# A graph-attention kernel on one core: three blocks of whole-array work in a batch, weights begun inside the last of them, the last batch's small work spread

## The chip, the core and the metric

The kernel runs on one NeuronCore of a Trainium2 chip. A core has five engines that run side by side, each through its own list of instructions: TensorE (PE, matrix products and transposes), VectorE (DVE), ScalarE (ACT), GpSimd (POOL) and SyncE (SP), which issues most of the DMAs. The metric is the time of one execution on the device in microseconds. Everything is float32.

## What is computed

Two layers, each followed by a residual addition and a layernorm. Layer 0 is a graph attention over 16 batches of 1024 nodes with 256 channels; layer 1 is a graph convolution with two linear layers and two batchnorms. The change lies in layer 0:

```python
fea = jnp.transpose(x, (0, 2, 1))
c_adj = jnp.mean(fea, axis=1)
diff = c_adj[:, None, :] - c_adj[:, :, None]
A = jnp.abs(jnp.abs(jax.nn.sigmoid(diff) - 0.5) - 0.5) * 2.0
A_s = (A + jnp.transpose(A, (0, 2, 1))) * 0.5
Wg = adj[None, :, :] * A_s
g = jax.nn.relu(jnp.einsum('bcn,bnm->bcm', fea, Wg) * para.reshape(1, C, N))
# q is g seen as 4 heads of 64 channels; k and v are the halves of x @ kv_w
attn = jax.nn.softmax(jnp.einsum('bhnd,bhmd->bhnm', q, k) * scale, axis=-1)
out = jnp.einsum('bhnm,bhmd->bhnd', attn, v)
x = _layernorm(x + out)
```

The weights of the graph depend on the differences of the nodes' channel means alone. In the kernel they come out as (tanh(|mean_i - mean_j| / 2) - 1) times the adjacency, and the sign goes into the scale of the queries.

## The kernel before, in words

Layer 0 is the first two thirds of the execution. Its work is a list of 512 units, 32 in a batch: batch b, pair of heads pr, half of the queries qh, and block m of 128 keys. Two units make a burst; a batch has 16 bursts, numbered u = 0 to 15. The two heads of a pair and the two halves of a key block are placed on the four 64 by 64 quadrants of TensorE, which compute side by side. For every burst the order is: `scores` (L903) of both its units into two score tiles of the "s" pool (two tiles of two PSUM banks each), each followed by its Exp on ScalarE (L908); then `back`, that is `outputs` (L924), of the burst before, whose additions of the exponentials to `acc` run on VectorE (L931, L933). So an Exp has the time of one `outputs` until the next scores want its tile. After the last key block the two output banks are put together in `oT` (ACT L937, then DVE L938).

All else on TensorE uses the whole 128 by 128 array, and is put between the bursts by hand: the order of TensorE, VectorE and ScalarE is exactly that of the program (`manual_schedule`). `prologue(b)` makes three lists for a batch, which are worked off one and two batches ahead:

- `first`: four transposes of x into xT (L765, with the copy L768). Ahead of the first stands `begin`: the channel sums (L747), the means and the negative means, a DMA that writes the 1024 negative means to DRAM (`c`, L754), and a second one that reads them back spread over all partitions (`crow`, L756). The second waits on SyncE until the first has landed.
- `steps`: the values (L855, 4 steps) and keys (L842, 4 steps), and `graph_mm` (L805, 16 steps), which multiplies x by the weights, half of the width at a time, into one-bank tiles of the "t" pool. After the last step of a half follow the product with `para` (DVE L814) and a Relu (ACT L817).
- `side`: the weights; for each of eight row blocks an Abs (L784) and a Tanh (L789) on ScalarE and a product with the adjacency (DVE L793). Abs reads `crow`. The eight weight tiles are freed by the last `graph_mm` that reads them.

`FULL` names the bursts with whole-array work: u = 0 and 4 take four steps of values and keys each, with two side steps after each; u = 6, 8, 10 and 12 take four steps of `graph_mm`; the transposes of `first` stand around those of u = 10 and 12. The remaining side steps stand at u = 13, 14, 15, 1, 2 and 3. The block of u = 6 is the first half width of the first 128 channels, and so on to u = 12.

Three dictionaries keyed by the burst hold what follows a pair of heads: `normalise` (L946 and L952: the denominators, four 128 by 32 products, copied and sent through DRAM into columns, L954 and L959) one burst later, `residual` (L967 to L979: reciprocal, transposes of oT, product, addition to x on POOL) five bursts later, and `finish_x1` six bursts later: `layernorm` wholly on VectorE (L596 to L600), with its square root on POOL, and a store of x1 by POOL. At u = 5, `load_x` reads the batch after the next into the slot of x that this store has freed.

In the last batch there is nothing to prepare. `last` puts there the transposes of the adjacency for layer 1 and other preparations; `before_last` puts row sums and the diagonal of the adjacency on VectorE in the batch before.

Of the kernel before, what the change touches and what calls it, by code (L numbers as in the profile page):

```python
# [18 lines left out]
P = 128  # L19
# [496 lines left out]
def fast_path(  # L516
# [86 lines left out]

    def products(name, bank, out, mm, temps, bias):
# [95 lines left out]
    with (  # L700
# [5 lines left out]
        tc.tile_pool(name="op", bufs=3) as op,  # L706
# [26 lines left out]
        def prologue(b):  # L733
# [24 lines left out]
            def transpose_x(c, half):  # L758
                if c == 0 and half == 0 and b:
                    begin()  # L760
# [7 lines left out]
                nc.vector.tensor_copy(s["xT"][:, c, half * HALF : (half + 1) * HALF], pt)  # L768
# [28 lines left out]
            def graph_mm(c, half, part):  # L797
                if part == 0:
                    s["pg"] = tile_t(f"pg_{b}_{c}_{half}")
                    if c == 0 and half == 0:  # L800
                        s["qT"] = qkv.tile([P, CC, N], F32, tag="qT", name=f"qT_{b}")
                ps = s["pg"]
                hs = slice(half * HALF, (half + 1) * HALF)
                for n in (2 * part, 2 * part + 1):
                    nc.tensor.matmul(  # L805
                        ps, xt[:, n, c * P : (c + 1) * P], s["wg", n][:, hs],
                        start=(n == 0), stop=(n == NCH - 1),
                    )
                if part == 3:
                    queries(c, hs, ps)  # L810
# [37 lines left out]
            def values(pair):  # L848
# [3 lines left out]
                for j in range(2):  # L852
# [6 lines left out]
                nc.vector.tensor_copy(  # L859
                    s["v"][:, 2 * pair : 2 * pair + 2, :].rearrange("p n c -> p (n c)"), pt  # L860
                )
# [3 lines left out]
            if b == 0:  # L865
                first += [(begin, ()), (row_of_means, ())]
            for i in range(4):
                step(values, i)
                step(keys, i // 2, i % 2)
            for c in range(CC):  # L870
                for half in range(2):
                    for part in range(4):
                        if b:
                            step(graph_mm, c, half, part)
# [105 lines left out]

        def finish_x1(b):
            xt = st.pop(b)["x"]
            layernorm(xt, f"l0_{b}")
            nc.gpsimd.dma_start(x1_d[b], xt)
# [125 lines left out]

        BURST = 2
        bursts = [range(i, i + BURST) for i in range(0, len(units), BURST)]
        PERB = PER // BURST
        FULL = (0, 4, 6, 8, 10, 12)
        SIDE = {13: 2, 14: 2, 15: 2, 1: 2, 2: 2, 3: 2}
        with tc.manual_schedule(engines={mybir.EngineType.PE, mybir.EngineType.Activation, mybir.EngineType.DVE}):
# [8 lines left out]
            run(next_first, 4)  # L1125
# [7 lines left out]
            full, sums, late = {}, {}, {}  # L1133

            def back(j):
# [4 lines left out]
                if m == NCH - 1 and qh == 1:  # L1140
                    sums.setdefault(j + 1, []).append((normalise, (b, pr)))
                    for q in range(2):
                        full.setdefault(j + 5, []).append((residual, (b, pr, q)))
                    if pr == PAIRS - 1:
                        late.setdefault(j + 6, []).append((finish_x1, (b,)))
# [14 lines left out]
                6: [(adjacency_rows, (n,)) for n in (0, 1, 2)] + [(load_weights, ())],  # L1160
                8: [(adjacency_rows, (n,)) for n in (3, 4, 5)],
                10: [(adjacency_rows, (n,)) for n in (6, 7)],
                12: [(adjacency_diagonal, ())],
            }
            for j in range(len(bursts)):
# [8 lines left out]
                run(late.get(j, []), 9)  # L1174
# [3 lines left out]
                if u in FULL:  # L1178
                    if u >= 10:
                        run(next_first, 1)  # L1180
                    for _ in range(4 if b or u > 4 else 0):
                        run(steps, 1)
                        if u <= 4:
                            run(side, 2)
                    if u >= 10:
                        run(next_first, 1)
                    run(full.get(j, []), 9)
                elif u > 12:
                    run(next_side, SIDE[u])
                else:  # L1190
# [441 lines left out]
```

## Time and profile before

| | us |
|---|---|
| median of three runs | 2638.08 (2633.52 to 2638.3) |
| the profiled execution's own time | 2637.64 |
| span of its trace | 2635.9 |
| TensorE idle within the span | 63.2 |
| scores L903, TensorE busy | 490.5 |
| outputs L924, TensorE busy | 485.3 |
| graph_mm L805, TensorE busy | 425.2 |
| Exp L908, ScalarE busy, mean of one | 495.6, 1.020 |
| additions L933, VectorE busy, mean of one | 483.2, 1.258 |
| weights L784 and L789, ScalarE busy | 146.6 and 135.5 |
| product with adjacency L793, mean of one | 1.217 |
| layernorm on VectorE: L596, L597, L600, mean of one | 0.397, 0.181, 0.407 |

The span runs from the first to the last instruction of the trace; the execution's own time also has what lies around it. The busy time of a group is the time in which at least one of its instructions ran. A matmul shows as two records, and the ends of matmuls are modelled, so their starts are what to compare. From 200 to 1600 us every stretch of 100 us looks alike: TensorE 99.4 busy, VectorE 62 to 69, ScalarE 50 to 55. Layer 0 ends near 1740 us; a batch takes 104.9 us (the write of the means L754 starts at 652.51, 757.42, 862.32 and 967.23).

### The profile page before, as it was taken

The page shows a single profiled execution, that of the slowest core. Times are in us where ns is not written, and L with a number is a line of the kernel's source. Part 1 is how long each engine was busy: PE and PEld are TensorE (multiplying, and loading weights), DVE is VectorE, ACT ScalarE, POOL GpSimd, SP SyncE. Part 2 cuts the span into 40 slices and gives each one's busy share as a digit, 9 for nine tenths or more (in the row PEclk, how much of TensorE's full clock was granted, in tenths as well). Part 3 has the DMA queues.
Part 4 walks back from the last instruction along what each step waited for, and adds up shares of the span by engine and source line. Part 5 has one row for each costly group of instructions (what it writes and reads, how often), then busy time and mean ns, then how long its engine had stood idle before and what let it go on. Part 6 is the DMA issues. An engine that isn't in the chain of part 4 may idle for free. (4 is left out here: it accounts for less than half of the span.)

```text
span 2635.9 us, 32325 instructions
## 1 busy us (share of the span) xinstructions
PE 2572.7 (98%) x13158; PEld 1118.6 (42%) x13158; DVE 1587.8 (60%) x2159; ACT 1110.2 (42%) x1321; POOL 338.9 (13%) x407
## 2 busy tenths in 40 slices
PE   8999999999999999999999999999999999999986
PEld 4443444444434444444344443334444444444455
DVE  5465665756656657566566576766565565533367
ACT  5363563644635636546356364501100111133358
POOL 0001000100000001001000010232221122000036
PEclk9999999999999999999999999999999999999999
DMA  4001101011011010110110110112222222254458
GB/s 144 2 9 41 33 10 41 17 25 33 9 41 33 10 41 19 23 33 9 41 33 9 41 49 2 41 55 89 96 76 84 86 90 96 96 201 150 159 194 303
DMA packets 134557, 168.96 MB, mean 64 GB/s; under 512 B 86784, under 2 KB 120064, under 8 KB 124032
## 3 DMA queue, kind: packets, MB, share of 16 engines
q1 hardware_dynamic: 129568, 116.47, 14.1%
q0 software_dynamic: 4832, 50.34, 4.6%
q8 instruction: 105, 1.72, 0.3%
q14 instruction: 52, 0.43, 0.0%
HBM read 99.36 MB, written 67.44 MB: 63 GB/s over the span
## 5 line engine op out<-in xcount | busy, mean ns | idle before, releaser
L908 ACT ACTIVATE p<-ps 128x1024 f32<-128x1024 f32 x512 | 495.6, 1020 | 179.7 <-PE ps L903 132.6
L933 DVE TENSOR_TENSOR acc<-acc,p 128x1024 f32<-128x1024 f32 x384 | 483.2, 1258 | 60.9 <-ACT p L908 32.3
L903 PE MATMUL ps<-qT,kT 64*64 64x512 f32 x4096 | 490.5, 594 | 1.4 <-ACT p L908 1.4
L924 PE MATMUL po<-p,v 64*64 64x512 f32 x4096 | 485.3, 589 | 0.0
L805 PE MATMUL pg<-wg,x 128*128 128x512 f32 x960 | 425.2, 596 | 0.0
L979 POOL TENSOR_TENSOR x<-x,o 128x512 f32<-128x512 f32 x64 | 109.5, 1711 | 1434.8 <-DVE o L974 1434.8
L924 PEld LDWEIGHTS po<-p,v 64*64 64x64 f32 x4096 | 156.7, 133 | 282.8 <-issue 282.6
L805 PEld LDWEIGHTS pg<-wg,x 128*128 128x128 f32 x960 | 177.6, 190 | 226.9 <-issue 203.3
L903 PEld LDWEIGHTS ps<-qT,kT 64*64 64x64 f32 x4096 | 146.1, 132 | 280.2 <-issue 231.5
L817 ACT ACTIVATE qT<-qT 128x512 f32<-128x512 f32 x64 | 40.1, 630 | 481.9 <-DVE qT L814 481.9
L1457 PE MATMUL po<-hl,w12T 128*128 128x512 f32 x512 | 222.0, 596 | 3.6 <-ACT hl L1387 2.8
L814 DVE SCALAR_TENSOR_TENSOR qT<-pg,para_s 128x512 f32<-128x512 f32 x64 | 43.9, 689 | 270.7 <-PE pg L805 269.8
L793 DVE SCALAR_TENSOR_TENSOR wg<-wg,adj_s 128x1024 f32<-128x1024 f32 x128 | 153.1, 1217 | 16.0 <-ACT wg L789 16.0
L1457 PEld LDWEIGHTS po<-hl,w12T 128*128 128x128 f32 x512 | 97.7, 191 | 127.9 <-issue 120.4
L784 ACT ACTIVATE wg<-crow,ccol 128x1024 f32<-128x1024 f32 x128 | 146.6, 1146 | 12.2 <-DMA crow<-c 12.2
L789 ACT ACTIVATE wg<-wg 128x1024 f32<-128x1024 f32 x128 | 135.5, 1059 | 2.6
L1387 ACT ACTIVATE hl<-hl,bn_sh,bn_sg 128x1024 f32<-128x1024 f32 x64 | 74.4, 1229 | 137.4 <-DMA hl<-h 136.1
L855 PE MATMUL pv<-kvw_s,xT 128*128 128x256 f32 x512 | 124.0, 385 | 1.6 <-ACT kT L846 1.6
L1468 DVE TENSOR_SCALAR o<-po,col_b 128x1024 f32<-128x1024 f32 x31 | 39.8, 1283 | 138.1 <-PE po L1457 138.1
L842 PE MATMUL pk<-xT,kvw_s 128*128 128x512 f32 x256 | 120.3, 592 | 0.0
L855 PEld LDWEIGHTS pv<-kvw_s,xT 128*128 128x128 f32 x512 | 94.9, 190 | 51.9 <-issue 27.6
L1286 PE MATMUL b_agg<-aT,x1S 128*128 128x512 f32 x240 | 109.2, 598 | 0.0
(159 smaller groups left out, 2641.4 us busy)
## 6 DMA issues: line engine op xcount, KB each, us to landing
h<-hw POOLq DMA_DIRECT2D x16, 2048.0 KB, 6.6
hl<-h SPq DMA_DIRECT2D x15, 2048.0 KB
x<-x POOLq DMA_DIRECT2D x16, 1024.0 KB, 4.2
x1l<-x SPq DMA_DIRECT2D x16, 1024.0 KB
xf<-x SPq DMA_DIRECT2D x16, 1024.0 KB
out_dram<-o SPq DMA_DIRECT2D x16, 1024.0 KB
x<-in_x_dram SPq DMA_DIRECT2D x15, 1024.0 KB
crow<-c SPq DMA_DIRECT2D x15, 512.0 KB
```

Source lines behind the costliest of these rows:

```text
L784: nc.scalar.activation(w, s["crow"], AF.Abs, bias=s["ccol"][:, n : n + 1])
L789: nc.scalar.activation(w, w, AF.Tanh, scale=0.5)
L793: nc.vector.scalar_tensor_tensor(w, w, 1.0, adj_s[:, n, :], op0=ALU.subtract, op1=ALU.mult)
L805: nc.tensor.matmul(ps, xt[:, n, c * P : (c + 1) * P], s["wg", n][:, hs], start=(n == 0), stop=(n == NCH - 1),)
L842: nc.tensor.matmul(ps, kvw_s[:, c, kc * P : (kc + 1) * P], s["xT"][:, c, hs], start=(c == 0), stop=(c == CC - 1),)
L855: nc.tensor.matmul(pt[:, j * C : (j + 1) * C], s["xT"][:, c, n * P : (n + 1) * P], kvw_s[:, c, C : 2 * C], start=(c == 0), stop=(c == CC - 1),
L903: nc.tensor.matmul(ps[kh * D : (kh + 1) * D, hd * HALF : (hd + 1) * HALF], kT[r, pr, ks], qT[r, pr, qh * HALF : (qh + 1) * HALF], start=Tr ...
L908: nc.scalar.activation(p, ps, AF.Exp)
L924: nc.tensor.matmul(g["po"][kh][hd * D : (hd + 1) * D, :], s["v"][r, m, h * D : (h + 1) * D], p[r, hd * HALF : (hd + 1) * HALF], start=(m = ...
L933: nc.vector.tensor_add(g["acc"], g["acc"], p)
L979: nc.gpsimd.tensor_tensor(xs, xs, o.rearrange("p n h d -> p n (h d)"), ALU.add)
L1457: nc.tensor.matmul(ps[:, hs], w2T[:, k, c * P : (c + 1) * P], h[k][:, hs], start=(k == 0), stop=(k == HC - 1),)
```

## The change

Layer 0's order between the bursts is written anew. The matrix products, their number and their sizes stay as they are.

- A batch has three blocks of whole-array work, at u = 0, 4 and 8. At u = 0: seven of the eight values and keys steps, the remaining side steps, the denominators of the second pair of the batch before, and all four residuals of the batch before. At u = 4: eight `graph_mm` steps (the first 128 channels at full width), then the last keys step. At u = 8: `begin`, two transposes, four `graph_mm` steps, two transposes, four `graph_mm` steps, the denominators of the first pair.
- `begin` is a step of its own, the first of `first`. The first four side steps of the batch after the next stand inside the block at u = 8, behind its sixth, seventh and eighth `graph_mm` step; from u = 9 on two and one side steps alternate.
- `graph_mm` takes one row block over the full width, into a tile of the "s" pool; the product with `para` and the Relu are done once over 1024 elements.
- The layernorm of layer 0 has two parts: `statistics` on VectorE and POOL at the head of u = 4, `apply` on ScalarE in its middle. Half of the copies of xT and of the values go from VectorE to ScalarE. `oT` has four buffers in place of three.
- In the batch before the last the row sums are spread over more bursts and the diagonal goes to u = 15. In the last batch the residuals stand at u = 2, 4 and 12, the layernorm's two parts at u = 5 and u = 7.
- `full`, `sums` and `late` are lists that are worked off in order.

```diff
+    def layernorm_steps(t, name):
+        st = small.tile([P, NCH, 6], F32, tag="ln_st", name=f"st_{name}")
+        mv = small.tile([P, NCH, 2], F32, tag="ln_mv", name=f"mv_{name}")
+        rstd = small.tile([P, NCH], F32, tag="ln_rs", name=f"rs_{name}")
+        nmr = small.tile([P, NCH], F32, tag="ccol", name=f"nm_{name}")
+        def statistics():
+            for n in range(NCH):
+                nc.vector.bn_stats(st[:, n, :], t[:, n, :])
+                nc.vector.bn_aggr(mv[:, n, :], st[:, n, :])
+            rsqrt(rstd, mv[:, :, 1], EPS)
+            nc.gpsimd.tensor_tensor(nmr, mv[:, :, 0], rstd, ALU.mult)
+            nc.gpsimd.tensor_scalar(nmr, nmr, -1.0, None, ALU.mult)
+        def apply():
+            for n in range(NCH):
+                nc.scalar.activation(
+                    t[:, n, :], t[:, n, :], AF.Identity,
+                    bias=nmr[:, n : n + 1], scale=rstd[:, n : n + 1],
+                )
+        return statistics, apply
...
-        tc.tile_pool(name="op", bufs=3) as op,
+        tc.tile_pool(name="op", bufs=4) as op,
...
             def transpose_x(c, half):
-                if c == 0 and half == 0 and b:
-                    begin()
...
-                nc.vector.tensor_copy(s["xT"][:, c, half * HALF : (half + 1) * HALF], pt)
+                copy = nc.scalar.copy if half and b else nc.vector.tensor_copy
+                copy(s["xT"][:, c, half * HALF : (half + 1) * HALF], pt)
...
-            def graph_mm(c, half, part):
-                if part == 0:
-                    s["pg"] = tile_t(f"pg_{b}_{c}_{half}")
-                    if c == 0 and half == 0:
+            def graph_mm(c, n):
+                if n == 0:
+                    s["pg"] = tile_s(f"pg_{b}_{c}")
+                    if c == 0:
                         s["qT"] = qkv.tile([P, CC, N], F32, tag="qT", name=f"qT_{b}")
-                ps = s["pg"]
-                hs = slice(half * HALF, (half + 1) * HALF)
-                for n in (2 * part, 2 * part + 1):
+                for hs in (H0, H1):
                     nc.tensor.matmul(
-                        ps, xt[:, n, c * P : (c + 1) * P], s["wg", n][:, hs],
+                        s["pg"][:, hs], xt[:, n, c * P : (c + 1) * P], s["wg", n][:, hs],
                         start=(n == 0), stop=(n == NCH - 1),
                     )
-                if part == 3:
-                    queries(c, hs, ps)
+                if n == NCH - 1:
+                    queries(c, slice(0, N), s["pg"])
...
-                nc.vector.tensor_copy(
-                    s["v"][:, 2 * pair : 2 * pair + 2, :].rearrange("p n c -> p (n c)"), pt
-                )
+                copy = nc.scalar.copy if pair % 2 and b else nc.vector.tensor_copy
+                copy(s["v"][:, 2 * pair : 2 * pair + 2, :].rearrange("p n c -> p (n c)"), pt)
...
             if b == 0:
                 first += [(begin, ()), (row_of_means, ())]
+            else:
+                first.insert(0, (begin, ()))
             for i in range(4):
                 step(values, i)
                 step(keys, i // 2, i % 2)
-            for c in range(CC):
-                for half in range(2):
-                    for part in range(4):
-                        if b:
-                            step(graph_mm, c, half, part)
+            for c in range(CC if b else 0):
+                for n in range(NCH):
+                    step(graph_mm, c, n)
...
+        def statistics_x1(b):
+            statistics, st[b]["ln"] = layernorm_steps(st[b]["x"], f"l0_{b}")
+            statistics()
         def finish_x1(b):
-            xt = st.pop(b)["x"]
-            layernorm(xt, f"l0_{b}")
-            nc.gpsimd.dma_start(x1_d[b], xt)
+            s = st.pop(b)
+            s["ln"]()
+            nc.gpsimd.dma_start(x1_d[b], s["x"])
...
-        FULL = (0, 4, 6, 8, 10, 12)
-        SIDE = {13: 2, 14: 2, 15: 2, 1: 2, 2: 2, 3: 2}
...
-            run(next_first, 4)
+            run(next_first, 5)
...
-            full, sums, late = {}, {}, {}
+            full, sums, late = [], [], []
...
                 if m == NCH - 1 and qh == 1:
-                    sums.setdefault(j + 1, []).append((normalise, (b, pr)))
+                    sums.append((normalise, (b, pr)))
                     for q in range(2):
-                        full.setdefault(j + 5, []).append((residual, (b, pr, q)))
+                        full.append((residual, (b, pr, q)))
                     if pr == PAIRS - 1:
-                        late.setdefault(j + 6, []).append((finish_x1, (b,)))
+                        late.append((statistics_x1, (b,)))
+                        late.append((finish_x1, (b,)))
...
             before_last = {
-                6: [(adjacency_rows, (n,)) for n in (0, 1, 2)] + [(load_weights, ())],
-                8: [(adjacency_rows, (n,)) for n in (3, 4, 5)],
-                10: [(adjacency_rows, (n,)) for n in (6, 7)],
-                12: [(adjacency_diagonal, ())],
+                6: [(load_weights, ())],
+                8: [(adjacency_rows, (n,)) for n in (0, 1, 2, 3)],
+                10: [(adjacency_rows, (4,))],
+                11: [(adjacency_rows, (5,))],
+                12: [(adjacency_rows, (6,))],
+                13: [(adjacency_rows, (7,))],
+                15: [(adjacency_diagonal, ())],
             }
...
-                run(late.get(j, []), 9)
                 if u == 5 and b + 2 < B:
                     load_x(b + 2)
                     next_first, next_steps, next_side = prologue(b + 2)
-                if u in FULL:
-                    if u >= 10:
-                        run(next_first, 1)
-                    for _ in range(4 if b or u > 4 else 0):
+                if b == B - 1:
+                    if u == 0:
+                        run(sums, 1)
+                    elif u in (2, 4, 12):
+                        run(full, 2)
+                    elif u == 5:
+                        run(late, 1)
+                    elif u == 7:
+                        run(late, 1)
+                    elif u == 8:
+                        run(sums, 1)
+                elif u == 0:
+                    for i in range(7):
+                        if b:
+                            run(steps, 1)
+                            run(side, 1 if i < 5 else 2)
+                        if i == 1:
+                            run(sums, 1)
+                        if i in (2, 3, 5):
+                            run(full, 1)
+                    run(side, 99)
+                    run(full, 1)
+                elif u == 4:
+                    run(late, 1)
+                    keys_last = steps[:1] if b else []
+                    del steps[: len(keys_last)]
+                    for n in range(NCH):
                         run(steps, 1)
-                        if u <= 4:
-                            run(side, 2)
-                    if u >= 10:
-                        run(next_first, 1)
-                    run(full.get(j, []), 9)
-                elif u > 12:
-                    run(next_side, SIDE[u])
-                else:
-                    run(side, SIDE.get(u, 0))
+                        if n == 3:
+                            run(late, 1)
+                    run(keys_last, 1)
+                elif u == 8:
+                    run(next_first, 3)
+                    for n in range(NCH):
+                        run(steps, 1)
+                        if n == 3:
+                            run(next_first, 2)
+                        if n > 4:
+                            run(next_side, 2 if n == 5 else 1)
+                    run(sums, 1)
+                elif u > 8:
+                    run(next_side, 1 + u % 2)
                 if b == B - 2:
                     run(before_last.get(u, []), 9)
                 if b == B - 1:
                     run(last.get(u, []), 9)
-                run(sums.get(j, []), 9)
...
                 aggregate_first(m)
-                run(sums.get(j + m - 1, []), 9)
-                run(full.get(j + m, []), 9)
+                if m == 1:
+                    run(sums, 1)
+                if m == 4:
+                    run(full, 2)
             for i in range(NCH // 2):
                 adjacency_sums(i)
-            run(late.get(j + 5, []), 9)
+            run(late, 2)
```

## The prediction, made before the changed kernel was run

> **What bounds the kernel now.** First the page's busy times, then TensorE alone in order of time over a batch, then ScalarE, VectorE and SyncE around the places that the change moves.
>
> ```profile
> span 2635.9 us, 32325 instructions
> PE 2572.7 (98%) x13158; PEld 1118.6 (42%) x13158; DVE 1587.8 (60%) x2159; ACT 1110.2 (42%) x1321; POOL 338.9 (13%) x407
> ```
>
> TensorE is the bound: only a microsecond of TensorE counts. In order of time (start, length, what, how many; two records per matmul):
>
> ```profile
> 720.91 1.95 PE L903 MATMUL ps<-qT,kT 64*64 64x512 f32 x16
> 722.68 1.90 PE L924 MATMUL po<-p,v 64*64 64x512 f32 x16
> 724.40 1.90 PE L903 MATMUL ps<-qT,kT 64*64 64x512 f32 x16
> 726.11 1.90 PE L924 MATMUL po<-p,v 64*64 64x512 f32 x16
> 727.94 7.13 PE L805 MATMUL pg<-wg,x 128*128 128x512 f32 x16
> 735.00 1.95 PE L903 MATMUL ps<-qT,kT 64*64 64x512 f32 x16
> ...
> 749.10 1.06 PE L946 MATMUL den<-acc,ones 128*32 128x512 f32 x8
> 750.09 1.95 PE L903 MATMUL ps<-qT,kT 64*64 64x512 f32 x16
> 751.86 1.90 PE L924 MATMUL po<-p,v 64*64 64x512 f32 x16
> ```
>
> A set of 16 quadrant records takes 1.717 us (722.68 to 724.40), a whole-array matmul 0.857. From 720.91 to 735.00 are 14.09 us; four sets and a block of eight matmuls should be 13.73. Going to whole-array work and back costs 0.365 us. A batch in mid run has six such blocks (u = 0, 4, 6, 8, 10, 12). A denominator behind a block adds 1.0 us.
>
> The row of means that ScalarE's weights read:
>
> ```profile
> 742.77 0.69 DVE L938 TENSOR_TENSOR oT<-po,oT 128x512 f32<-128x512 f32 x1 [1.47 <-ACT oT L937]
> ...
> 754.84 2.28 DVE L747 TENSOR_REDUCE csum<-x 128x8 f32<-128x2048 f32 x1
> ...
> 757.42 0.36 SPq L754 DMA_DIRECT2D c<-ncol  x1
> 766.14 0.34 SPq L756 DMA_DIRECT2D crow<-c  x1
> ...
> 784.57 1.16 ACT L784 ACTIVATE wg<-crow,ccol 128x1024 f32<-128x1024 f32 x1
> 785.76 1.06 ACT L789 ACTIVATE wg<-wg 128x1024 f32<-128x1024 f32 x1
> ```
>
> Here is the price to see: the 4 KB write of the means is issued at 757.42, and the read that spreads it over the partitions only 8.72 us later. In 13 batches this gap is 8.7 to 11.2 us, mean 10.1. The read's traffic then ends 2.9 to 5.1 us after its issue (windows of half a microsecond, four batches). Both together took 13.5, 13.9, 15.0 and 15.2 us there: 14.4. Nobody waits for it now; the first weight starts 27 us after the write's issue.
>
> **What the Trainium skill says.** "TensorEngine Tiling (Array Packing)", Key Properties: changing the tiling mode drains the array. The 0.365 us agree. "DMA: Bandwidth & Descriptors", Rules for kernel authors: a strided last dimension becomes one descriptor per element. The write of 1024 single values, slower than the 512 KB read, agrees. "TensorE: Matmul & The Clock Gate", What's actually happening: after an idle window of about 3.4 us the clock is halved until a busy window has passed. The trace is stricter: idle from 1757.9 to 1759.95 was enough.
>
> ```profile
> 1758.00:1760.00 2.00, 0.12 (x2) 0.05 (x1) 1.91 (x6) 0.00 (x0) 0.46 (x1) 1.00 0.00 0
> 1760.00:1762.00 2.00, 2.00 (x3) 0.90 (x4) 1.12 (x2) 0.00 (x0) 0.17 (x1) 0.63 0.68 283
> 1762.00:1764.00 2.00, 2.00 (x4) 0.80 (x3) 0.31 (x1) 0.00 (x0) 0.00 (x0) 0.52 0.64 250
> ```
>
> (Stretch, its length, busy PE, PEld, DVE, ACT, POOL, then the granted clock.) A half clock through these 3.4 us loses 1.7 us of work.
>
> **Part 1, three blocks.** Batches 1 to 14 lose three blocks each, batch 0 two (four to two); the last batch gains one, its residual at u = 2. 14 x 3 + 2 - 1 = 43 round trips x 0.365 = -15.7 us. The matmuls stay the same. A graph block now fills a two-bank score tile for 16 x 0.857 = 13.7 us; VectorE's product over 1024 elements (about 1.25 us by the 1024-wide L793 rows) and ScalarE's Relu (about 1.0) replace two pairs of half width. At u = 4 the last keys step (1.7 us of TensorE) hides the product before the second score needs the tile: nothing.
>
> **Part 2, the block at u = 0.** Seven values and keys steps, one denominator, four residuals. The denominator now stands between whole-array steps and pays a second mode change: not shown in the trace; between 0 and 0.3 us, I take 0.2 (the gap that a denominator has ahead of it), x 14 = +2.8. The two-buffer small tiles need a copy within each 1.7 us step, while weights (1.15 and 1.06 us) stand before it on ScalarE. I count three waits of 0.25 to 0.3 us, against 0.24 at u = 4 and 0.35 at u = 12 now: between -0.6 and +0.6, I take +0.25, x 14 = +3.5. The denominators' columns come back about 4 us after the row copy, and the third residual stands 7 us behind it: hidden.
>
> **Part 3, layernorm to ScalarE, copies shared.** VectorE loses 8 x 0.41 us, four copies of 0.69 and the wait for POOL (2.1 us); ScalarE gains 8 x about 0.5, plus four copies of 0.58; POOL two tiny operations. All lies inside the 13.7 us block at u = 4: statistics to T4+5.8, POOL to 8.9, ScalarE to 13.2, before the Relu at 15.2. The store (4.2 us to landing) and then the load of x (issued when the store has landed, done 5 us later) end at T4+23; the next reader is the block at u = 8, T4+29.4. Hidden with 6 us to spare. At the start, ScalarE's copies of xT wait behind weights: +1.
>
> **Part 4, weights inside the block at u = 8.** Call the block's start T (742.03 in the trace). TensorE: four transposes of 0.49, 16 matmuls, T+15.7; denominator and change, T+16.9; two scores (1.77) and the outputs (1.72), T+20.35. Then the first score of the next burst needs the tile that the Exp of this burst's first score frees.
> VectorE reaches `begin()` after the oT addition, T+1.43; reduction and small ones 2.58: write issued at T+4.0; row landed at T+18.4 (17.5 to 19.2). ScalarE's order is written by hand: abs 0 (waits for the row), tanh 0, abs 1, Relu, tanh 1, denominator row, and only then the Exps of u = 9. 1.20 + 0.96 + 1.1 + 0.95 + 0.96 + 0.5 + 1.02 = 6.7 us, so the first Exp ends at T+25.1. TensorE waits 25.1 - 20.35 = 4.8 us. Without any wait for the row the Exp would end near T+20.8, 0.4 late; the row would have to be there by T+13.6. What is queued behind the waiting abs is the whole attention. Afterwards ScalarE has 2.0 us of Exps and one weight step (1.1) per burst of 3.43, and catches up. It happens in batches 0 to 13, which have a batch after the next: 14 x 4.8 = +67.
> Such a gap will bring the half clock. Part of the 3.4 us lies in the gap itself: between 0 and 3.4 us of loss per gap, I take 1.2, x 14 = +17. SP's queue also holds the read for 10 us; the denominators' DMAs behind it are used at u = 0, long after.
>
> **Part 5, last batch.** VectorE's diagonal and rows are spread: the 1.08 us wait at 1627 goes. The layernorm at u = 7 puts 4 us of ScalarE before the Exps and the transposed copies of u = 8: +1.9 (0 to 2.5). At the end VectorE no longer waits for POOL in the layernorm, which held u_h until 1759.95: -1.9 (0 to -3.6 with its half clock). Net -1.1.
>
> **Sum.** Against the profiled execution's 2637.6 us (span 2635.9; the runs' median is 2638.1): -15.7 + 2.8 + 3.5 + 1 - 1.1 = -9.5; +67 +17: 2712 us.
>
> **Rivals.** A, above: the row is late. For it: the chain's parts are all measured; against: no run shows it under this order. The row at its earliest without the clock's loss gives 2628 + 14 x 3.9 = 2683, the row at its latest with 2 us of clock 2735.
> B, the other side: the row comes in time, by T+13.6, because the scattered write lands in under 5.3 us (9.6 for write and read together, where 14.4 is measured); then TensorE keeps its mode changes: 2628 plus up to 0.4 x 14, about 2631. For it: the write's time varies by 2.5 us from batch to batch, so it is not fixed by its size alone. Against: none of 13 was faster than 8.7.
>
> C, the clock decides: every gap opens two half windows, 3 us each: 2628 + 14 x 7.8 = 2737. Against: the dip shown above lasted one window, (0.37 + 0.48) x 2 / 0.5 = 3.4 us.
>
> **How the numbers follow.** A 0.75, B 0.15, C 0.10. Likeliest is A: 2712, its own range 2683 to 2735. For 8 in 10, 2660 to 2737. A measurement here tells 0.2% (5 us): B is 0.10 faster and 0.05 same (its 2631 is only 6.6 us below), A and C are slower.
>
> **What would show it.** Right: ScalarE idle before L784's first weight in the middle of the run, released by the DMA of crow, 5 to 6 us; TensorE idle 4 to 6 us once per batch before scores, two sets after the denominator; a clock below 1 there; three 128*128 blocks per batch. Wrong: crow on the chip before the sixth of the block's matmul steps, or a wait that VectorE's tile copies cause at u = 0.

## The result, and the profile after

The changed kernel takes 2726.11 us (2725.38 to 2726.76); the kernel before took 2638.04 beside it. The ratio is 1.034, with a 95% interval of 1.0327 to 1.0352: slower by 88 us. The profiled spans differ by 89.0 us.

From the page of the changed kernel: its size, the busy times, then the chain that ended last (shares of the span by engine and by line), then two groups (busy, mean ns of one, idle before it and its releaser).

```profile
span 2724.9 us, 32314 instructions
PE 2600.7 (95%) x13158; PEld 1130.8 (41%) x13158; DVE 1515.7 (56%) x1941; ACT 1208.5 (44%) x1479; POOL 349.6 (13%) x439
...
PE 72%; DVE 10%; DMA 8%; ACT 7%; issue 2%; POOL 0%; ACTq 0%; DVEq 0%; POOLq 0%; SPq 0%
...
L924 PE MATMUL ps<-qT,kT 64*64 64x512 f32 x4096 | 515.0, 618 | 61.7 <-ACT p L929 61.3
...
L808 ACT ACTIVATE wg<-crow,ccol 128x1024 f32<-128x1024 f32 x128 | 146.5, 1146 | 129.4 <-DMA crow<-c 129.4
```

The same two groups on the page of the kernel before:

```profile
L903 PE MATMUL ps<-qT,kT 64*64 64x512 f32 x4096 | 490.5, 594 | 1.4 <-ACT p L908 1.4
L784 ACT ACTIVATE wg<-crow,ccol 128x1024 f32<-128x1024 f32 x128 | 146.6, 1146 | 12.2 <-DMA crow<-c 12.2
```

TensorE has the same 13158 records of matmuls, but its busy time has grown by 28.0 us: the same work at a lower clock. The scores wait 61 us for an Exp, where they waited 1.4, and the weights on ScalarE wait 129 us for the row of means, where they waited 12. In the chain that ended last DMAs have 8%: the way of that row runs through it.

The timeline of TensorE in the changed kernel around one block at u = 8 (start, length, what; in brackets the idle time before it and what ended it):

```profile
787.60 1.10 PE L788 MATMUL pxT<-ident,x 128*128 128x128 f32 x8
...
803.24 1.06 PE L967 MATMUL den<-acc,ones 128*32 128x512 f32 x8
804.24 1.95 PE L924 MATMUL ps<-qT,kT 64*64 64x512 f32 x16
806.00 1.90 PE L945 MATMUL po<-p,v 64*64 64x512 f32 x16
812.88 3.69 PE L924 MATMUL ps<-qT,kT 64*64 64x512 f32 x16 [4.98 <-ACT p L929]
816.35 3.05 PE L945 MATMUL po<-p,v 64*64 64x512 f32 x16
819.23 1.89 PE L924 MATMUL ps<-qT,kT 64*64 64x512 f32 x16
```

What the wait hangs on, in the same timeline on VectorE, SyncE's queue and ScalarE:

```profile
788.95 2.28 DVE L772 TENSOR_REDUCE csum<-x 128x8 f32<-128x2048 f32 x1
...
791.53 0.36 SPq L779 DMA_DIRECT2D c<-ncol  x1
802.33 0.34 SPq L781 DMA_DIRECT2D crow<-c  x1
...
806.27 1.15 ACT L808 ACTIVATE wg<-crow,ccol 128x1024 f32<-128x1024 f32 x1 [9.21 <-DMA crow<-c]
807.45 1.06 ACT L813 ACTIVATE wg<-wg 128x1024 f32<-128x1024 f32 x1
808.41 1.13 ACT L808 ACTIVATE wg<-crow,ccol 128x1024 f32<-128x1024 f32 x1
809.45 1.04 ACT L839 ACTIVATE qT<-qT 128x1024 f32<-128x1024 f32 x1
810.40 1.04 ACT L813 ACTIVATE wg<-wg 128x1024 f32<-128x1024 f32 x1
811.35 0.56 ACT L973 COPY drow<-den 128x512 f32<-128x512 f32 x1
811.81 1.93 ACT L929 ACTIVATE p<-ps 128x1024 f32<-128x1024 f32 x2
```

Read from the block's start T = 787.60: write issued at T+3.9, read at T+14.7, the first weight (Abs) at T+18.7. The five ScalarE instructions behind it that are not Exps run without a break, and the first Exp of u = 9 ends near 812.8, T+25.2. TensorE had been done with the outputs at 806.00 + 1.72 = 807.72 and starts the scores at 812.88: a gap of 5.16 us. ScalarE's lines show the reason in one bracket: 9.21 us idle, ended by the DMA of crow.

The clock at the same place, in windows of the changed kernel (stretch, length, busy PE, PEld, DVE, ACT, POOL, granted clock, DMA share, GB/s):

```profile
807.72:811.85 4.13, 0.18 (x4) 0.00 (x0) 1.23 (x1) 4.13 (x6) 0.00 (x0) 1.00 0.00 0
811.85:812.88 1.03, 0.00 (x0) 0.00 (x0) 0.02 (x1) 1.03 (x3) 0.00 (x0) 0.50 0.01 2
812.88:818.68 5.80, 5.80 (x28) 1.78 (x32) 4.64 (x4) 4.89 (x5) 0.00 (x0) 0.50 0.19 3
818.68:820.00 1.32, 1.32 (x16) 0.43 (x12) 1.32 (x2) 0.00 (x0) 0.00 (x0) 1.00 0.00 0
```

The clock is full for the first 4.13 us of the gap, falls to 0.50 at 811.85, 1.03 us before the work resumes, and is full again at 818.68. Of the 6.83 us at half clock 5.80 lie behind the gap, and half of these are lost: the two sets there take 3.47 us (812.88 to 816.35) and 2.88 us (816.35 to 819.23) in place of 1.72 each, 2.9 us more, on top of the gap.

All batches with such a gap, 0 to 13, added up from the starts of the sets: the gaps are 4.1 to 5.5 us, 63.5 in all (mean 4.5); the six sets behind each gap lose 1.6 to 3.0 us, 33.0 in all (mean 2.4). Together that is 96.5 us, while the spans differ by 89.0; so all the rest of the change brings -7.5. In five of these batches the clock falls within 0.3 us of the work's return and stays low for 3.41 us; in nine it falls 0.9 to 2.0 us before it and stays low for 6.83.

### The profile page after: what moved, and what is told of

It reads as the page before. It is cut to its first block, busy times and chain, and to the rows that moved or that the text cites. A ratio compares the mean times of both kernels' runs of the same rounds, so it can differ in the third digit from the quotient of the medians.

```text
span 2724.9 us, 32314 instructions
## 1 busy us (share of the span) xinstructions
PE 2600.7 (95%) x13158; PEld 1130.8 (41%) x13158; DVE 1515.7 (56%) x1941; ACT 1208.5 (44%) x1479; POOL 349.6 (13%) x439
## 3 DMA queue, kind: packets, MB, share of 16 engines
q1 hardware_dynamic: 129568, 116.47, 13.6%
q8 instruction: 105, 1.72, 0.3%
## 4 chain that ended last, share of the span: by engine, by line
PE 72%; DVE 10%; DMA 8%; ACT 7%; issue 2%; POOL 0%; ACTq 0%; DVEq 0%; POOLq 0%; SPq 0%
PE ps L924 16%; PE po L945 15%; PE pg L827 8%; PE po L1514 8%; DMA c<-ncol 5%; PE pv L877 4%; PE pk L864 4%; PE b_agg L1343 4%; PE c_agg L1343 4%; DMA crow<-c 2%; PE b_h L1375 2%; PE a_agg L1343 2%; PE c_h L1375 1%; ACT wg L813 1%; DVE csum L772 1%
## 5 line engine op out<-in xcount | busy, mean ns | idle before, releaser
L924 PE MATMUL ps<-qT,kT 64*64 64x512 f32 x4096 | 515.0, 618 | 61.7 <-ACT p L929 61.3
L945 PE MATMUL po<-p,v 64*64 64x512 f32 x4096 | 496.5, 599 | 0.0
L924 PEld LDWEIGHTS ps<-qT,kT 64*64 64x64 f32 x4096 | 152.1, 137 | 362.3 <-issue 255.7
L817 DVE SCALAR_TENSOR_TENSOR wg<-wg,adj_s 128x1024 f32<-128x1024 f32 x128 | 163.5, 1280 | 53.9 <-ACT wg L813 53.9
L836 DVE SCALAR_TENSOR_TENSOR qT<-pg,para_s 128x1024 f32<-128x1024 f32 (+1 forms) x34 | 39.2, 1161 | 236.0 <-PE pg L827 235.0
L959 DVE TENSOR_TENSOR oT<-po,oT 128x512 f32<-128x512 f32 x64 | 44.3, 691 | 155.1 <-ACT oT L958 155.1
L622 ACT ACTIVATE x<-x,nm_l,rs_l 128x256 f32<-128x256 f32 x128 | 64.6, 587 | 111.4 <-POOL nm_l L618 111.4
```

Of the source, the lines that this page charges most:

```text
L817: nc.vector.scalar_tensor_tensor(w, w, 1.0, adj_s[:, n, :], op0=ALU.subtract, op1=ALU.mult)
L924: nc.tensor.matmul(ps[kh * D : (kh + 1) * D, hd * HALF : (hd + 1) * HALF], kT[r, pr, ks], qT[r, pr, qh * HALF : (qh + 1) * HALF], start=Tr ...
L945: nc.tensor.matmul(g["po"][kh][hd * D : (hd + 1) * D, :], s["v"][r, m, h * D : (h + 1) * D], p[r, hd * HALF : (hd + 1) * HALF], start=(m = ...
```

## The experiments

Three questions. Is the time of `begin` the cause, and is its effect a threshold with a slope of one behind it, or does weights' work inside the block cost by itself? How much of the loss is the clock? And what became of the mode changes that the change saves? Each diff is against the changed kernel unless it says otherwise. Ratios are to the kernel before, with their 95% intervals.

**Begin two bursts earlier.** The weights stay where the change put them.

```diff
+                elif u == 6:
+                    run(next_first, 1)
                 elif u == 8:
-                    run(next_first, 3)
+                    run(next_first, 2)
```

> Changed kernel with one edit: begin (sums, the write of the means, the read of the row) stands at u = 6 instead of the head of u = 8; the weights stay inside the block. Theory A (the row of means is late): the write is issued about 3 us before the block instead of 4 us after it, the row lands at about T+11.3, before the limit of T+13.6. The 61 us of TensorE idle time before scores and the 34 us lost to the half clock go; ScalarE's work ahead of the Exps of u = 9 leaves 0.4 to 0.5 us per batch: 2726 - 95 + 7 = 2638, between 2631 and 2641. Rival (crowding: it is the amount of ScalarE work put before the Exps, two Abs, two Tanh, a wide Relu, that stalls, whenever the row comes): the wait stays at 3 us or more per batch, 2690 to 2726.

Measured: 2638.19 us, ratio 1.0002 (0.9994 to 1.001). The write is issued at 746.73, and this is what follows in the timeline of ScalarE and TensorE of this kernel, where the block at u = 8 starts at 750.92:

```profile
762.26 1.15 ACT L808 ACTIVATE wg<-crow,ccol 128x1024 f32<-128x1024 f32 x1 [1.88 <-DMA crow<-c]
...
769.32 1.90 PE L945 MATMUL po<-p,v 64*64 64x512 f32 x16
771.37 2.00 PE L924 MATMUL ps<-qT,kT 64*64 64x512 f32 x16 [0.16 <-ACT p L929]
```

ScalarE still waits 1.88 us for the row, but from T+11.3 on it runs, and TensorE goes on at 771.37, 0.33 late. The 96.5 us have become 6.2 (4.7 and 1.5 by the same sums). One step moved takes back the whole loss, and nothing more: the time is that of the kernel before.

**Begin one burst earlier.** The same with `u == 7`.

> The same edit at half the distance: begin at u = 7. Theory A: write issued at about T+0.3, row at T+14.0 to 15.7, so 0.2 to 2 us of wait per batch (about 1.1), too short for the half clock in most batches: 2726 - 95 + 15 = 2646, between 2635 and 2665. Crowding: as in the changed kernel, 2690 to 2726.

Measured: 2637.6 us, 1.0003 (0.9995 to 1.0012). In SyncE's and ScalarE's timeline of this kernel:

```profile
747.46 0.36 SPq L779 DMA_DIRECT2D c<-ncol  x1
...
764.01 1.15 ACT L808 ACTIVATE wg<-crow,ccol 128x1024 f32<-128x1024 f32 x1 [3.94 <-DMA crow<-c]
```

The time lies in the range expected, but its premise missed. I had put the write just behind the block's start, but at u = 7 VectorE has not yet reached the addition into oT, which at u = 8 stands ahead of the sums: the reduction runs at 744.88, and the write leaves at T-3.2 (T = 750.61). In this batch, the latest of the 14, the first weight starts at T+13.4, just ahead of the T+13.6 that the prediction gave as the limit; the gap is 0.34 as at u = 6.

**Begin later**, behind the second pair of transposes in the middle of the block.

```diff
                 elif u == 8:
-                    run(next_first, 3)
+                    x_first = next_first[1:]
+                    del next_first[1:]
+                    run(x_first, 2)
...
-                            run(next_first, 2)
+                            run(x_first, 2)
+                            run(next_first, 1)
```

> The changed kernel with begin later instead of earlier: behind the fifth and sixth transposes' copies in the middle of the block, so that VectorE comes to it at about T+9 instead of T+1.4. Theory A: every microsecond that the row comes later is one of TensorE's: 7.7 us more per batch, 14 x 7.7 = 108, the half clock's part about the same: 2726 + 108 = 2834 (2815 to 2850). If the wait has a part that doesn't depend on the row, less.

Measured: 2836.48 us in a single run, 110.4 above the changed kernel. The gaps sum to 171.3 us (11.7 to 13.2 each), 107.8 more than in the changed kernel, which is 7.7 a batch, as much as was put ahead of `begin`; the loss behind them to 34.7, 1.7 more. The gap follows the row one to one, and the clock's part does not grow with it. Two windows of one of these gaps (855.57 to 868.52) show why:

```profile
859.94:868.52 8.58, 0.00 (x1) 0.01 (x1) 1.25 (x2) 6.59 (x8) 0.00 (x0) 0.50 0.13 49
868.52:873.59 5.07, 5.07 (x24) 1.53 (x28) 3.91 (x4) 4.24 (x5) 0.00 (x0) 0.50 0.23 3
```

The clock falls 4.37 us after the gap's start and stays low through the rest of it, where that costs nothing; only the 5.07 us behind the gap cost time.

**Begin where the change put it, the weights outside the block**, two in each burst from u = 9.

```diff
-                        if n > 4:
-                            run(next_side, 2 if n == 5 else 1)
...
                 elif u > 8:
-                    run(next_side, 1 + u % 2)
+                    run(next_side, 2)
```

> Changed kernel, but no weights inside the block at u = 8: begin stays at its head, and the side steps start at u = 9, two in every burst. Theory A and crowding both: nothing on ScalarE waits for the row ahead of the Exps of u = 9, the gap and the half clock go; ScalarE then has up to 4.2 us of work in bursts of 3.43 at u = 9 and 10, 0 to 0.5 us per batch: 2631 to 2640. A rival in which the gap comes from the long score tile or from the block itself: 2690 to 2726.

Measured: 2639.51 us, 1.0009 (1.0002 to 1.0015). No gap behind the block (-0.01 in every batch). So a row that is late costs nothing as long as no instruction ahead of the Exps asks for it; about 0.5 us comes in the later bursts instead.

**Is it the clock?** Five matmuls stand in the gap, into a spare tile.

```diff
                 elif u > 8:
+                    if u == 9 and b + 2 < B:
+                        fill = tile_t(f"fill_{b}")
+                        for _ in range(5):
+                            nc.tensor.matmul(fill, ident, adj_s[:, 0, H0], start=True, stop=True)
```

> Changed kernel with five more matmuls (identity times 512 columns of the adjacency, into a small tile that nobody reads) between the outputs and the scores where TensorE waits at u = 9: 5 x 0.857 + 0.365 for the two mode changes = 4.65 us, where the wait is 3.9 to 5.3 us. The row stays late. Theory A with the clock: TensorE doesn't idle, the clock stays at 1.0, the 34 us of half clock come back, 14 x 0.3 to 0.5 us are added by the filling that is longer than the wait: about 2698 (2690 to 2706). If the half clock cost nothing (its time hidden behind ScalarE): 2726 to 2734.

Measured: 2709.18 us, 1.0273 (1.0258 to 1.0289), 16.9 below the changed kernel. TensorE's timeline in this kernel, at the same block:

```profile
801.84 4.56 PE L1250 MATMUL fill<-adj_s,ident 128*128 128x512 f32 x10
807.84 2.00 PE L924 MATMUL ps<-qT,kT 64*64 64x512 f32 x16 [1.44 <-ACT p L929]
809.66 1.90 PE L945 MATMUL po<-p,v 64*64 64x512 f32 x16
811.38 1.90 PE L924 MATMUL ps<-qT,kT 64*64 64x512 f32 x16
```

Behind the filled gap the sets start 1.82 and 1.72 us apart. Over 14 batches the loss behind the gaps is 3.2 us in place of 33.0, and 1.8 of it is one batch whose wait was still 2.27 us. That the clock takes some 30 us is shown. The time fell by less, because the gaps themselves grew from 63.5 to 77.4, where I had expected 6 us more. In every batch the scores still wait 0.2 to 2.3 us for the Exp behind the dummies, so the dummies are nowhere longer than the wait: it is the row that came later. From the write's issue to the first weight are 15.1 us on average in this run, in the changed kernel 14.1, and 14 x 1.0 is the whole growth. The dummies don't seem to delay it: the kernels with `begin` at u = 6 and 7, measured on the same chip, have as slow a write (at its quickest 9.0 to 9.4 us until the read, in the changed kernel 8.5 to 8.8).

**What became of the saved mode changes.** With `begin` at u = 6 the kernel is level with before, though it has three blocks less in a batch. The timeline of TensorE in the changed kernel, within the block at u = 0, shows where they went:

```profile
733.92 0.60 PE L991 MATMUL poT<-ident,oT 128*128 128x128 f32 x4
734.76 1.98 PE L864 MATMUL pk<-xT,kvw_s 128*128 128x512 f32 x4 [0.24 <-ACT v L882]
736.58 0.60 PE L991 MATMUL poT<-ident,oT 128*128 128x128 f32 x4
737.42 2.00 PE L877 MATMUL pv<-kvw_s,xT 128*128 128x256 f32 x8 [0.24 <-ACT kT L868]
```

From a residual's transposes to the next step are 0.84 us, and the waiting step then takes 1.82 until its successor, where another takes 1.72. A residual's four transposes are only 0.43 us of TensorE, so the next step asks for a small tile before ScalarE's copy has freed it.

Two edits in turn mend this. The first, on `begin` at u = 6, takes the Tanh that stands behind the Relu ahead of it, so that the Exps come sooner:

```diff
-                        if n > 4:
-                            run(next_side, 2 if n == 5 else 1)
+                        if n in (5, 6):
+                            run(next_side, 2)
```

> begin_u6 with the fourth weight step (Tanh 1) ahead of the Relu of the block instead of behind it, two side steps after the sixth and two after the seventh matmul step. In begin_u6 TensorE still waits 0.34 us before the second scores behind the block, and the scores then start up 0.11 us slower, in each of 14 batches. Theory (the last of the ScalarE work ahead of the Exps): the wait goes, 14 x 0.45 = -6 us: about 2632. If the wait is the row's or the wide tile's: no change, 2638.

Measured: 2630.66 us, 0.9976 (0.9967 to 0.9985); the batch's period falls from 104.85 to 104.41 us. The second gives the residuals of u = 0 a bank of the outputs, which are idle there, in place of a small tile (`residual` takes the pool as an argument):

```diff
-            pt = tile_t(f"poT_{k}")
+            pt = (bank or tile_t)(f"poT_{k}")
...
-                        if i in (2, 3, 5):
-                            run(full, 1)
+                        if i in (2, 3, 4, 5):
+                            for f, a in full[:1]:
+                                f(*a, bank=tile_o)
+                            del full[:1]
                     run(side, 99)
-                    run(full, 1)
```

> u6_side, and at u = 0 the four residuals use the two output banks, which are empty there, instead of the two small tiles, and stand one behind each of the third to sixth step. Theory: the gain of the three mode changes, 1.1 us per batch, is given back in begin_u6 at u = 0, where three steps wait for a small tile; each wait shows 0.24 us but with the restart behind it costs 0.46. Without them 14 x 3 x 0.46 = -19 us: about 2613. Rival: the mode changes simply don't pay what the trace of before showed (0.365 us each), and the waits cost what they show: 14 x 0.72 = -10: 2622.

Measured: 2610.35 us, 0.9896 (0.9881 to 0.9912). The same place in TensorE's timeline of this kernel:

```profile
685.42 0.60 PE L991 MATMUL poT<-ident,oT 128*128 128x128 f32 x4
685.86 1.88 PE L864 MATMUL pk<-xT,kvw_s 128*128 128x512 f32 x4
687.58 0.60 PE L991 MATMUL poT<-ident,oT 128*128 128x128 f32 x4
688.01 1.89 PE L877 MATMUL pv<-kvw_s,xT 128*128 128x256 f32 x8
```

0.44 us in place of 0.84, then 1.72 in place of 1.82: 0.50 for each of three waits, and the period falls by 1.51 us, to 102.90. Each wait was printed as 0.24. Now the kernel with three blocks is 27 us below the kernel before (2637.71 beside it).

**What one block more costs**, on the kernel just told: in batches 1 to 14 the last values step stands alone at u = 2.

```diff
+                elif u == 2:
+                    if b:
+                        run(steps, 1)
...
-                        if b:
+                        if b and i < 6:
                             run(steps, 1)
+                        if b:
```

> u6_side_bank with a fourth block in batches 1 to 14: the last values step (four matmuls, 1.7 us) leaves the block at u = 0 and stands alone at u = 2; all else stays. It measures the price of one more way to whole-array work and back by itself. At the 0.365 us read from the trace of before: 14 x 0.365 = +5.1 us over u6_side_bank, 2615.5. If the mode change costs nothing and the gaps belonged to waits: +0.

Measured: 2623.57 us, 0.9951 (0.9938 to 0.9965): 13.2 us more, where 5.1 were expected. By the starts on TensorE the round trip is about 0.36 us a batch (0.20 of it from the lone values step to the next scores, 705.38 to 707.30 less 1.72), as before. The other 0.6 to 0.7 lie between the block at u = 0 and the lone step: four sets take 7.72 us (697.66 to 705.38) where 6.87 would do. VectorE and TensorE's weight loads (PEld) show the cause:

```profile
699.33 0.69 DVE L995 TENSOR_TENSOR o<-poT,r_all 128x512 f32<-128x512 f32 x1 [1.28 <-POOL x L1000]
...
699.43 0.13 PEld L945 LDWEIGHTS po<-p,v 64*64 64x64 f32 x1 [0.30 <-issue]
700.07 0.63 PEld L945 LDWEIGHTS po<-p,v 64*64 64x64 f32 x11 [0.51 <-DVE o L995]
```

The first outputs behind the block want the bank that the last residual still holds. Its product on VectorE has waited for POOL and ends at 700.02, so most of the set can go on only at 700.07, some 0.65 us late; this wait stands in all 14 batches. With the longer block that product ends at 694.79 and the outputs come at 695.93. So, by the trace, the price of a block itself is the 0.36; the rest is the price of lending the bank.

**The layernorm back on VectorE**, on the same kernel: `apply` as four vector operations in place of ScalarE's.

```diff
-                nc.scalar.activation(
-                    t[:, n, :], t[:, n, :], AF.Identity,
-                    bias=nmr[:, n : n + 1], scale=rstd[:, n : n + 1],
+                nc.vector.tensor_scalar(
+                    t[:, n, :], t[:, n, :], mv[:, n, 0:1], rstd[:, n : n + 1], ALU.subtract, ALU.mult
```

> u6_side_bank with the second part of layer 0's layernorm on VectorE again (eight of 0.41 us) instead of ScalarE (4.0 us), at the same place in the block at u = 4. The prediction held that work in the 13.7 us of this block is hidden on either engine: no change in batches 1 to 14; at the end of layer 0 VectorE waits for POOL again (+1.9, and a half clock of up to 1.7), and in the last batch ScalarE is relieved at u = 8 (-1.3): 2610 to 2614.

Measured: 2608.84 us, 0.9893 (0.9878 to 0.9908), a little below the range, but no gain can be told from 2610.35: two of its four runs take 2606.4, the other two 2611.2 and 2611.6. A batch in mid run takes 102.90 us on either engine: the engine of the layernorm decides nothing there.

**The last batch, in two ways**, on the same kernel. First its residuals in small tiles at u = 0, 4, 6 and 8, the denominators behind the transposes of the adjacency, the layernorm at u = 9 and 11:

```diff
-                    if u == 0:
-                        run(sums, 1)
-                    elif u in (2, 4, 12):
+                    if u in (0, 4, 6, 8):
+                        run(full, 1)
+                    elif u == 12:
                         run(full, 2)
...
+                    if u in (0, 8):
+                        run(sums, 1)
```

> u6_side_bank with another last batch: its first denominators stand behind the transposes again, its four old residuals one each in the blocks of u = 0, 4, 6 and 8 (no extra block at u = 2, no second residual that waits for POOL), the layernorm at u = 9 and 11. In the changed kernel this batch has 1.35 us ahead of half of the denominators, 2.7 us before the transposes of u = 4 with a half clock behind them (1.2), one extra block (0.37) and 1.3 at u = 8. Expected -3 to -6 us: about 2608.

Measured: 2611.2 us, 0.9901 (0.9886 to 0.9916): nothing gained. The batch's last outputs start 3.3 us sooner (1679.62, before 1682.91), and this is given back behind them: VectorE is late with the scaled adjacency, and TensorE waits 1.05 and 2.41 us for it, where it waited 1.33 once. Then the residuals two at a time at u = 0, 4 and 12 in banks of the outputs, the layernorm where the change has it:

```diff
-                    if u == 0:
-                        run(sums, 1)
-                    elif u in (2, 4, 12):
-                        run(full, 2)
+                    if u in (0, 4, 12):
+                        for f, a in full[:2]:
+                            f(*a, bank=tile_o)
+                        del full[:2]
```

> u6_side_bank with another last batch than all_mended: the four old residuals at u = 0 and u = 4 and two at u = 12, all in the empty output banks, so that the transposes beside them keep the small tiles; denominators behind the transposes; statistics at u = 5 and apply at u = 7 as in the changed kernel, so that VectorE isn't late at the end, which is what took all_mended's gain. Of u6_side_bank's last batch 1.35 us ahead of the denominators, 1.9 to 2.7 before the transposes of u = 4, up to 3 of half clock and one block (0.37) should go: -4 to -7, 2603 to 2606.

Measured: 2606.42 us (2606.1 to 2607.04), 0.9886 (0.9871 to 0.9901). Layer 1's first products start 1.9 us sooner (1682.83, before 1684.76), and the wait of 1.33 us within them is gone. The kernel beats the one before by 31 us and the changed one by 120, by the medians. What the change lost by was where it put two things, a row of means and four residuals. How much of the 31 us is due to the three blocks isn't shown, for the banks were not tried in the kernel before. Its six blocks stand about 1.0 us a batch above their mode changes (3.2 against 2.2, as worked out below), so I estimate that up to 14 us might have been had there without a new order.

## Why the prediction was right, point by point

The side, the mechanism and the range held. The forecast was 74 us above the profiled execution; 88 were measured.

- **Part 4, the row.** Each stage of the chain came as worked out, in the batch shown: write at T+3.9 (forecast 4.0), weight at T+18.7 (18.4; 17.6 to 19.0 over the batches), first Exp done at T+25.2 (25.1), TensorE free at T+20.1 (20.35). The gap's mean is 4.5 us (4.8), its sum 63.5 (67): from the write's issue to the first weight are 14.1 us on average (14.4). ScalarE's idle time before that weight is 8.1 to 9.5 us, not the 5 to 6 named as a sign: its last copy ahead of that weight ends at T+9.5. That moves nothing. That the row's lateness is the cause, with a limit near T+13.6 and slope one behind it, is shown by the four places of `begin`.
- **Part 4, the clock.** This is the term that was mis-sized: 1.2 us a gap were taken, 2.4 measured, 17 against 33 us. I took part of the low window to lie within the gap, and one window to be all. Part of it does lie there, but where that part is 0.9 to 2.0 us, in nine of 14 batches, a second window follows, so that 4.9 to 5.9 us of half clock are left behind the gap; in the other five hardly any of the window lies in the gap, and 3.1 to 3.4 are left. I had reckoned with 2.4. In those nine batches rival C, which asked for 3 us each time, was nearly right.
- **Parts 1 and 2, blocks and tiles.** The net is near (the sum of all other parts -7.5 against -9.5), but by luck: its two terms were both too small. In a batch in mid run the six blocks of before stand some 3.2 us above the bare sum of their work, not 2.2: their own small-tile waits went with them. The three blocks of after cost 2.7: 2.1 at u = 0 and 0.3 to 0.4 at each of the others. That is 0.5 saved a batch, 7 us in 14. The three waits at u = 0 were foreseen in number and printed length (0.24), but each costs 0.50. The denominator between whole-array steps costs 0.23 (0.2 taken). The sign named as proof of an error, a wait there for VectorE's copies, did not come: all three wait for ScalarE's.
- **Part 3, layernorm and copies.** Hidden, as said: in the changed kernel the eight operations of `apply` on ScalarE lie at 766.47 to 770.5, inside the block at u = 4, and neither engine for it moves the time.
- **Part 5, last batch.** The 1.08 us wait is gone, and so is the 1.88 us wait for u_h with its low clock. From the start of layer 1's first products (1801.07, before 1708.24) to the program's end 3.8 us are gained, just past the far end of the range given for them. Within the batch new waits came: 0.30 for the first denominator, 1.90 and 0.78 near 1745 with a low clock behind them, 1.15 at 1769. By subtraction (92.8 us at the start of those products, less 96.5, and plus the 7 that the blocks save) the batch is some 3 us longer, with the start of the program in it; the net is about -0.5, against -1.1 and +1 for the start.
- **Rival B** asked for the row by T+13.6. With `begin` at u = 7 that was met, and the time was 2637.6, not B's 2631: the first Exp is still 0.45 us late in each of 14 batches (6.3 us; B took half), and parts 1 and 2 bring 2 us less than forecast.

## What to carry to other kernels

Before an instruction is moved ahead of others on an engine that works in order, find the latest of its operands, and ask when that one's own chain can start at its new place: here a chain of reduction, write and read was started at the head of a block of 16 us, ended 18.7 us behind that head, and was wanted at 13.6. Once a gap on TensorE reaches about two microseconds, add the clock to it, and by the measured loss (here 1.4 to 3.0 us a gap), not by the gap's length. And where long steps are put together with short ones on a ring of two small tiles, look at the shortest step: it decides whether the copies keep up.

## What the runs showed of the hardware

- **The clock steps on a fixed grid of 3.413 us, and the loss follows from it.** Behind the 14 gaps of the changed kernel every stretch at half clock lasts 3.41 or 6.83 us, and their starts lie whole multiples of 3.413 us apart: 699.21, 811.85 and 924.49 are 33 steps from one another. The Trainium skill, "TensorE: Matmul & The Clock Gate", section "What's actually happening", says that the window is free-running; the grid agrees with it. The loss is half of the low time behind the gap: 1.6 to 1.7 us in five batches, 2.5 to 3.0 in nine. Gaps of 11.7 to 13.2 us cost hardly more than gaps of 4.1 to 5.5 (34.7 and 33.0 us in 14 batches), since most of the low time lies within them.
- **What counts is the idle time within one window.** Along that grid the 13 traces of this case have about 9,800 windows (without the first 60 us and the last 20). At full clock, the next window came at half clock after every window with more than 1.91 us of printed idle time, and after none with less than 1.69. At half clock, the next window came at full clock after every one with less than 0.55 us of idle time, and after none with 0.6 or more. This is why a second low window follows where the first begins 0.9 us or more before the work. It is also why one wait of 2.27 us in the kernel with the filled gap brought the half clock (all of it lay in one window), and one of 1.81 in the last kernel did not (1.73 of it lay in one). The same page asks for an idle window of about 3.4 us; here less was enough.
- **A wait costs more than it is printed with.** 0.24 us printed, 0.50 by the starts of the instructions around it and by the time of the kernel that lacks it. Of the difference 0.16 lie in the printed, modelled length of the transposes ahead (0.60, where the next step can start after 0.44), 0.10 in a slower step behind the wait.
- **A scattered write of 4 KB has two durations.** From the issue of the write of 1024 single values to that of the read behind it are 8.5 to 8.8 us in seven batches of the changed kernel and 10.3 to 10.9 in the other seven, and nothing between. With `begin` at u = 6 they are 9.1 to 9.4 and 10.8 to 12.0. It is not chance: batches 4, 6, 7 and 12 to 15 are the quick ones in all 12 kernels with the new order, batches 2, 3, 5, 8, 10 and 11 in the kernel before. What it hangs on is open. The read takes part of it back: in the changed kernel the first weight follows the write's issue by 13.8 us on average in the quick batches and 14.4 in the others, 0.7 sooner and not 2.
